# Layer 1's short scan: one length for each set of four states, and all sets of a group in one tile

## The chip, the cores and the metric

The kernel runs on one core of a Trainium2 chip. The metric is device time in microseconds. Three runs of the kernel before gave 12742.89, 12820.02 and 12823.61 us; their median is 12820.02 us.

Five engines work side by side, each through its own instructions in order, and wait for one another by semaphores: PE (matrix multiply, its results go to PSUM), DVE (vector operations and scans), ACT (activations and copies), POOL (vector operations on SBUF) and SP, which issues most of the DMA transfers here.

## The reference

Two layers of a state space model in two dimensions work on 8 images of 64 x 64 positions and 96 channels. Both normalize the image by groups, project it to 192 channels, convolve 3 x 3 by channel, and scan the 4096 positions in four directions with 16 states for each channel. A gated projection and a sum follow. Layer 0 has an ordinary recurrence. Layer 1 computes its scan by cumulative sums:

```python
dt = softplus(dt @ dt_proj_w + dt_proj_b)
A = -exp(A_log)                      # rates 1 to 16 in each channel
log_dA = einsum('bld,dn->bldn', dt, A)
dB_u = einsum('bld,bln->bldn', dt, B_mat) * u[..., None]
decay = exp(cumsum(log_dA, axis=1))
h = decay * cumsum(dB_u / (decay + 1e-12), axis=1)
y = einsum('bldn,bln->bld', h, C_mat) + u * D_skip
```

`decay` falls from position to position until it underflows to zero; from there on `h` is zero and only `u * D_skip` is left. So only the head of each of the four directions has to be scanned. How long the head must be depends on the sum of dt and on the rate of the state.

## The kernel before

**The long scan.** For layer 0, a step is one *set*: 4 of the 16 states of 32 channels on the 128 partitions, over 1024 positions. Four sets (`NS`) with the same channels are a *group*, three groups a *job* (96 channels, half `h`), and two jobs a *unit* (1024 positions in one direction). One image has 16 units, that is 384 sets.

`scan_rows` emits the work of all engines by hand, one set number n after another. For set n, DVE makes the drive and scans (`advance_set`); ACT makes the decay of set n+1 into PSUM (`fill`); POOL multiplies the states of set n-1 by C (`read_out`); PE sums the states of set n-3 into PSUM (`collect`); ACT takes the finished sums out (`release`). In the last set of a long group, POOL makes the drive instead of DVE (`early`, by `by_gpsimd`). SP fetches a group's replicated dt and dt*u from DRAM five sets ahead (`fetch`; two buffers each), and the rows of B and C four sets ahead (`replicate`; nine buffers in all). What prepares a job two jobs ahead (`ready`, `short_ready`) and the convolutions of other images (`conv_beside`) hang in a plan by set number; the numbers in the lists that these functions return are steps after the job's start. The matmuls of all planned stages share one bank (`pmisc`).

**The short scan.** Behind the long scan of images 1 to 7 stands one more unit, `short`: layer 1's scan of the image before. It scans a head of `HEAD` = 160 positions in each of the four directions. The four heads lie in one row of 640 columns (`HN`). The two heads of the backward directions are scanned from right to left, so that two scan instructions of 320 columns do a set; at the two joins dt is set to 1e30, which makes the decay zero there. The drive is first multiplied by 1 + tanh(...) of the summed dt (`gate`, and L838 in `advance_set`); this and the later factor 0.5 take the place of the division. The short unit has 2 jobs of 3 groups of 4 sets: 24 steps.

`short_ready` prepares a short job. It computes dt by softplus in several ACT steps, multiplies by u on POOL (`product`), sums dt along each head on DVE (`running`, L732, four scans of 160 columns into the buffer `dt0`), and keeps in `worst` the smallest product of a head's sum and the smallest rate (`lowest`). `store` at step 15 writes dt, dt*u and the sums to DRAM.

`worst` is compared with 104.5 (`GONE`) at the end of the program. If it is lower, a general scan of layer 1 is run for all images (`general_second`).

After the scan of an image, `between` finishes both layers' outputs (`out_phase`), where the matrix `avg` is loaded anew each time; the short scan's results come from DRAM (`ys_far`). The last image's layer 1 is done by `scan_head`, outside `scan_rows`.

Of the kernel before, what the change touches and what calls it, by code (L numbers as in the profile page):

```python
# [13 lines left out]
LATE = "in0", "in1", "cw0", "cw1", "cb0", "cb1", "spread", "avg", "pick"  # L14
# [24 lines left out]
CUTS = slice(0, MM), slice(MM, HN)  # L39

# [7 lines left out]
def two_ss2d_layers(ctx: ExitStack, tc: tile.TileContext, t: dict, out: bass.AP):  # L48
# [45 lines left out]
    nc.gpsimd.memset(one_col, 1.0)  # L94
    log_eps = const.tile([P, 1], F32, name="log_eps")
# [286 lines left out]
    def scan_parts(b):  # L382
# [20 lines left out]
        if b >= 1:  # L403
            unit = dict(short=True, nth=None, n=HN, b=b - 1)
            units.append(unit)
            for h in range(NH):
                jobs.append(dict(unit=unit, h=h))
                for g in range(NG):
                    group = dict(unit=unit, job=jobs[-1], h=h, g=g)
                    sets += [dict(unit=unit, group=group, i=i, first=False) for i in range(NS)]  # L410
# [3 lines left out]
    def scan_rows(xc, y, parts, plan, rows, beside):  # L414
# [10 lines left out]
        with (  # L425
# [11 lines left out]
            with tc.manual_schedule():  # L437
                state = None
                plan.setdefault(-1, []).insert(0, lambda: low_rows(x_dbl, units[1], rows))
                for n in range(-AHEAD, max(total + 4, max(plan, default=0) + 1)):  # L440
# [14 lines left out]
                    fetch(at(AHEAD), loads, work)  # L455
                    replicate(at(AHEAD_BC), x_dbl, loads)
                    if at(0) and at(0)["unit"]["nth"] == 0 and at(0)["first"]:
                        state = piece.tile([P, D // GC * NS], F32, name="state0", bufs=2)
# [3 lines left out]
                    if n % NS == NS - 2:  # L462
                        drive(at(2), pdrive)
                    release(at(-4), y, beside)
# [8 lines left out]
    def fetch(s, loads, work):  # L473

        if s and s["i"] == 0:
            group, n = s["group"], s["unit"]["n"]
            for c in ("dt", "dtu", "cum") if s["unit"]["short"] else ("dt", "dtu"):
                pool, size = (work, HN) if c == "cum" else (loads, T)
                group[c] = pool.tile([P, size], F32, name=f"{c}_rep")[:, :n]
# [3 lines left out]
    def replicate(s, x_dbl, loads):  # L483

        if s and s["group"]["h"] == 0 and s["group"]["g"] == 0:
            unit, n = s["unit"], s["unit"]["n"]
            if unit["short"]:
                rows, first = unit["far"], R
            else:
                rows = x_dbl[unit["k"] % 2][unit["k"] // 2 * ROWS :, unit["t0"] : unit["t0"] + T]  # L490
                first = R + 1
            for c, at in (("b", first), ("c", first + N)):
                rep = loads.tile([P, T], F32, tag="bc_rep", name=f"{c}_rep", bufs=2 * NS + 1)
                src = rows[at + GS * s["i"] :, :][:GS, :]
                nc.sync.dma_start(rep[:, :n], src.unsqueeze(0).broadcast_to([GC, GS, n]))
                unit[c, s["i"]] = rep[:, :n]
# [144 lines left out]
    def short_projection(xc, x_dbl, unit, piece, pmisc):  # L641


        def product(s):
            unit["ps"] = pmisc.tile([P, MM], F32, tag="mm", name="ps_short")
            at = CUTS[s]
# [9 lines left out]
        def take(s):  # L656
            if s == 0:
                unit["x_dbl"] = piece.tile([2 * ROWS, T], F32, name="x_dbl0")
            at, m = CUTS[s], R + 2 * N
            nc.scalar.copy(unit["x_dbl"][:m, at], unit["ps"][:m, : at.stop - at.start])  # L660
            if s == len(CUTS) - 1:
                unit["far"] = dram.tile([m, HN], F32, name="x_dbl1_short", bufs=2)
                nc.sync.dma_start(unit["far"], unit["x_dbl"][:m, :HN])
# [8 lines left out]
    def short_ready(xc, x_dbl, job, piece, pmisc):  # L672

        unit, h = job["unit"], job["h"]

        def bank(s, name):
            job["ps"] = pmisc.tile([P, MM], F32, tag="mm", name=name)
            return job["ps"][:C, : CUTS[s].stop - CUTS[s].start]

        def tile_of(name):  # L680
            return piece.tile([C, T], F32, name=name)[:, :HN]

        def argument(s):
            job["v"] = bank(s, "ps_dt1")
            lhs = w["dtw1"][:, 0, h * C : (h + 1) * C]
            nc.tensor.matmul(job["v"], lhs, unit["x_dbl"][:R, CUTS[s]], start=True, stop=True)

        def parts(s):
# [3 lines left out]
            nc.scalar.activation(job["dt"][:, CUTS[s]], job["v"], AF.Relu, bias=bias)  # L692
            nc.scalar.activation(job["z"][:, CUTS[s]], job["v"], AF.Abs, bias=bias)
# [15 lines left out]
        def total(s):  # L709
            job["v"] = bank(s, "ps_sp1")  # L710
            for i, term in enumerate(("z", "dtu", "ln", "dt")):
# [3 lines left out]
                    job[term][:, CUTS[s]],  # L715
# [4 lines left out]
        def delta(s):  # L720
            nc.scalar.copy(job["ln"][:, CUTS[s]], job["v"])
# [4 lines left out]
        def running():  # L726
            job["cum"] = tile_of("dt0")
            for k in range(K):
                d = slice(k * HEAD, (k + 1) * HEAD)
                if k >= 2:  # L730
                    d = slice(d.stop - 1, d.start - 1, -1)
                nc.vector.tensor_tensor_scan(  # L732
                    job["cum"][:, d],
                    one_col.to_broadcast([C, HEAD]),
                    job["ln"][:, d],
                    0.0,
                    ALU.mult,
                    ALU.add,
                )

        def lowest():
            last = small.tile([C, K], F32, name="last_short")
            for half in range(2):
                at = slice(HEAD - 1, 2 * HEAD, HEAD) if half == 0 else slice(2 * HEAD, HN, HEAD)
                nc.vector.tensor_scalar(
                    last[:, 2 * half : 2 * half + 2],
                    job["cum"][:, at],
                    w["least1"][:, h : h + 1],
                    None,
                    ALU.mult,  # L750
                )
# [4 lines left out]
        def store():  # L756

            nc.gpsimd.memset(job["ln"][:, JOINS], 1e30)
            job["dt"] = job["ln"]
            for c in ("dt", "dtu", "cum"):  # L760
                job[f"{c}_far"] = dram.tile([C, HN], F32, name=f"{c}_short", bufs=3)
# [7 lines left out]
            (3, exponential),  # L769
            (4, rounded),  # L770
            (5, rounding),
            (6, logarithm),
            (10, lambda: total(0)),
            (11, lambda: delta(0)),
            (11, lambda: total(1)),
# [1121 lines left out]
```

## Time and profile before

| What | Value |
|---|---|
| Median of 3 runs | 12820.02 us |
| Profiled execution, its own time | 12769.01 us |
| Its span in the profile | 12767.2 us |
| Instructions | 135071 |
| DVE busy | 11381.4 us (89%) |
| POOL busy | 10760.4 us (84%) |
| ACT busy | 9761.7 us (76%) |
| PE busy | 9506.2 us (74%) |
| Mean granted clock of PE | 0.788 |
| DMA queue of SP | 1818.14 MB, 43.2% of 16 engines |

All times in the profile come from the one profiled execution. A line such as L838 is a line of the kernel before. A group's line ends with the idle time of the engine just before its instructions, and with what ended that idle time. The lines of the order of instructions begin with the start and the length of an instruction in us; `<-` names output and input, and brackets hold an idle time and what ended it.

### The profile page before, as it was taken

Reading aid. Unit: us, or ns where it says so; the run is one execution under the profiler, and the core shown is the slowest. Engines: PE = TensorE matmul, PEld = TensorE weight load, DVE = VectorE, ACT = ScalarE, POOL = GpSimd, SP = SyncE. Lnnn points to the kernel's source line nnn. Section 1 sums busy time; section 2 is a strip of 40 time slices with the busy share of each in tenths; the row PEclk is TensorE's granted clock in tenths of the full one; section 3 lists DMA queues with packets and bytes.
Section 4 is the critical chain, followed back from the end, with each engine's and each line's share of the span. In section 5 each row is a group of like instructions: output and inputs, shape, how many; then the busy total and the mean of one; then the engine's idle time right before and its main releaser. Section 6 shows DMA issues by size and latency. Waiting matters only on the chain. (4 is left out here: it accounts for less than half of the span.)

```text
span 12767.2 us, 135071 instructions
## 1 busy us (share of the span) xinstructions
PE 9506.2 (74%) x44284; PEld 2996.9 (23%) x44284; DVE 11381.4 (89%) x7387; ACT 9761.7 (76%) x14977; POOL 10760.4 (84%) x4884
## 2 busy tenths in 40 slices
PE   5875588876887778876788758888588885886556
PEld 1221122222222222222222212222122221222112
DVE  6999799997999979999799987999889998899976
ACT  4888688776887768887788867888678886788864
POOL 3999799986999869998799977999779997899964
PEclk8877788777888778887788878878688877887766
DMA  3444444443444444444444435444344443444430
GB/s 97 161 161 155 133 164 162 160 139 117 164 161 160 142 128 164 156 156 132 133 161 161 158 119 155 150 152 159 122 151 161 159 152 117 146 159 159 153 98 25
DMA packets 653802, 1839.49 MB, mean 144 GB/s; under 512 B 174408, under 2 KB 177870, under 8 KB 652989
## 3 DMA queue, kind: packets, MB, share of 16 engines
q1 hardware_dynamic: 645917, 1818.14, 43.2%
q10 hardware_dynamic: 7168, 12.59, 0.3%
q8 instruction: 352, 5.77, 0.2%
q14 instruction: 365, 2.99, 0.1%
HBM read 1524.94 MB, written 305.52 MB: 143 GB/s over the span
## 5 line engine op out<-in xcount | busy, mean ns | idle before, releaser
L863 POOL TENSOR_TENSOR out<-set,c_rep 128x1024 f32<-128x1024 f32 x3240 | 7467.8, 2323 | 977.9 <-DVE set L846 307.5
L846 DVE TENSOR_TENSOR_SCAN set<-decay,state,set 128x1024 f32<-128x1024 f32 x2304 | 5365.2, 2345 | 390.1 <-ACT decay L801 151.6
L801 ACT ACTIVATE decay<-dt_rep,w_a 128x1024 f32<-128x1024 f32 x3240 | 3553.5, 1097 | 574.9 <-DVE set L846 334.5
L835 DVE TENSOR_TENSOR set<-drive,b_rep 128x1024 f32<-128x1024 f32 x2430 | 2865.2, 1179 | 15.9 <-ACT drive L818 9.0
L887 PE MATMUL acc<-out,w_gather 128*32 128x256 f32 x25920 | 2393.2, 481 | 546.8 <-ACT y_short L907 394.5
L955 PE MATMUL ps_conv<-edged,taps 96*96 96x512 f32 (+1 forms) x4032 | 2460.1, 749 | 29.8 <-ACT z L569 26.1
L825 POOL TENSOR_TENSOR set<-dtu_rep,b_rep 128x1024 f32<-128x1024 f32 (+1 forms) x810 | 1896.4, 2341 | 75.3 <-DMA dt_far<-ln 30.0
L846 DVE TENSOR_TENSOR_SCAN set<-decay,set 128x1024 f32<-128x1024 f32 x768 | 1744.3, 2286 | 167.7 <-ACT decay L801 87.8
L878 PE MATMUL acc<-map,w_eye 96*32 96x256 f32 x4608 | 566.8, 573 | 1471.7 <-ACT map L918 1237.3
L918 ACT COPY map<-acc 32x256 f32<-32x256 f32 x3072 | 1469.6, 478 | 48.3 <-PE acc L887 7.7
L887 PEld LDWEIGHTS acc<-out,w_gather 128*32 128x32 f32 x25920 | 839.4, 132 | 2519.4 <-issue 1455.0
L955 PEld LDWEIGHTS ps_conv<-edged,taps 96*96 96x96 f32 (+1 forms) x4032 | 722.8, 199 | 1371.0 <-issue 1230.3
L857 ACT COPY state<-set 128x1 f32<-128x1 f32 x2304 | 426.2, 185 | 752.1 <-DVE set L846 745.0
L588 PE MATMUL ps_sp<-z,w_eye 96*96 96x512 f32 x960 | 657.5, 773 | 292.7 <-ACT ln L597 245.0
L609 POOL TENSOR_TENSOR dtu<-ln,map 96x1024 f32<-96x1024 f32 x256 | 670.5, 2619 | 232.6 <-DVE ln L605 132.1
L818 ACT COPY drive<-dtu_rep 128x1024 f32<-128x1024 f32 (+1 forms) x810 | 797.2, 984 | 33.4 <-DVE x_in L1559 13.4
L556 PE MATMUL ps_dt<-x_dbl,w_dtw 7*96 7x512 f32 x1024 | 595.6, 663 | 219.6 <-ACT z L569 151.7
L588 PE MATMUL ps_sp<-dtu,w_eye 96*96 96x512 f32 x960 | 561.0, 669 | 0.0
L878 PEld LDWEIGHTS acc<-map,w_eye 96*32 96x32 f32 x4608 | 101.7, 122 | 1929.7 <-ACT map L918 1631.5
L588 PE MATMUL ps_sp<-ln,w_eye 96*96 96x512 f32 x960 | 540.8, 647 | 0.0
L588 PE MATMUL ps_sp<-dt,w_eye 96*96 96x512 f32 x960 | 507.8, 611 | 0.0
L597 ACT COPY ln<-ps_sp 96x512 f32<-96x512 f32 x480 | 278.7, 581 | 279.0 <-PE ps_sp L588 272.0
(228 smaller groups left out, 9621.6 us busy)
## 6 DMA issues: line engine op xcount, KB each, us to landing
dt_rep<-dt_far SPq DMA_DIRECT2D x768, 512.0 KB
dtu_rep<-dtu_far SPq DMA_DIRECT2D x768, 512.0 KB
b_rep<-x_dblr SPq DMA_DIRECT2D x256, 512.0 KB
c_rep<-x_dblr SPq DMA_DIRECT2D x256, 512.0 KB
b_rep<-x_dblc SPq DMA_DIRECT2D x256, 512.0 KB
c_rep<-x_dblc SPq DMA_DIRECT2D x256, 512.0 KB
dt_far<-ln SPq DMA_DIRECT2D x256, 384.0 KB
dtu_far<-dtu SPq DMA_DIRECT2D x256, 384.0 KB
```

Of the source, the lines that this page charges most:

```text
L588: nc.tensor.matmul(job["ps"][:C, :], w["eye"], job[term][:, halves[s]], start=i == 0, stop=i == 3,)
L609: nc.gpsimd.tensor_tensor(like(job["dtu"], col), like(job["dt"], col), positions(xc[:, h, :], col, t0, T), ALU.mult,)
L801: nc.scalar.activation(s["decay"], s["group"]["dt"], AF.Exp, scale=rate)
L818: nc.scalar.copy(s["group"]["drive"], s["group"]["dtu"])
L825: nc.gpsimd.tensor_tensor(s["buf"], s["group"]["dtu"], b, ALU.mult)
L835: nc.vector.tensor_tensor(s["buf"], s["group"]["drive"], b, ALU.mult)
L846: nc.vector.tensor_tensor_scan(ordered(s["buf"], unit), ordered(s["decay"], unit), ordered(s["buf"], unit), 0.0 if unit["nth"] == 0 else s ...
L863: nc.gpsimd.tensor_tensor(s["out"], s["buf"], s["unit"]["c", s["i"]], ALU.mult)
L878: nc.tensor.matmul(acc, lhs[:, GC * g : GC * (g + 1)], positions(old[:, h, :], unit["column"], unit["t0"] + at, n), start=True, stop=False ...
L887: nc.tensor.matmul(acc, w["gather"], s["out"][:, at : at + n], start=s["i"] == 0 and unit["short"], stop=s["i"] == NS - 1, skip_group_chec ...
L918: nc.scalar.copy(yk, like(acc, unit["column"]))
L955: nc.tensor.matmul(job["ps"][:C, :], taps[l][:k, h, tap, :], edged[:k, tap // 3 : tap // 3 + rows, tap % 3 : tap % 3 + WW], start=tap == 0 ...
```

## The change

Each set of four states gets a head of its own: 160, 40, 24 and 16 positions (`HEADS`). The smallest rate is taken for each set too (`least1`), so that the test of `worst` covers each set with its own length.

- The heads of all four sets of a group lie in one tile of 960 columns (`HT`): two halves of 480 (`BLOCK`), one for the forward and one for the backward directions; in each half the two heads of 160, then the two of 40, of 24 and of 16. A group of the short unit is now one step, not four: the unit has 6 steps.
- Decay and tanh use a different rate for each set, so ACT makes each of them in four pieces (`blocks`). The drive, the gated product, the two scans (480 columns each) and the read-out each do the whole tile. In the short unit the drive is always made by DVE.
- The ends of the convolved image are copied once more into the places of the shorter heads (`extend`, 12 small ACT copies per image). The projections and softplus of the short unit work on 960 columns.
- `running` uses two scans of 320 columns with a tile that has a zero at the second head's start. The products in `lowest` move from DVE to ACT (8 small ones per job).
- The stages of `short_ready` move up: `store` stands at step 11. It sets seven joins on POOL, where it was one instruction.
- Fetches of the short unit are issued two steps ahead; the sums use the buffers of B and C. B and C are loaded by four DMAs each.
- PE sums the four sets of a group by 16 matmuls of 160 to 16 columns. `release` is one ACT copy per group, and four stores to DRAM.
- For images 1 to 6 the convolutions beside the two last long jobs start at step 9.
- `avg` stays in SBUF.

The diff, cut to its core:

```diff
-LATE = "in0", "in1", "cw0", "cw1", "cb0", "cb1", "spread", "avg", "pick"
+LATE = "in0", "in1", "cw0", "cw1", "cb0", "cb1", "spread", "pick"
...
+HEADS = HEAD, 40, 24, 16
+OFFSETS = [2 * sum(HEADS[:i]) for i in range(len(HEADS))]
+BLOCK = 2 * sum(HEADS)
+HT = 2 * BLOCK
...
-                    sets += [dict(unit=unit, group=group, i=i, first=False) for i in range(NS)]
+                    sets.append(dict(unit=unit, group=group, i=0, first=False))
...
-                    fetch(at(AHEAD), loads, work)
+                    fetch(at(AHEAD), False, loads)
+                    fetch(at(2), True, loads)
                     replicate(at(AHEAD_BC), x_dbl, loads)
+                    replicate_short(at(AHEAD_BC), "b", loads)
+                    replicate_short(at(AHEAD_BC - 1), "c", loads)
...
-                    if n % NS == NS - 2:
-                        drive(at(2), pdrive)
-                    release(at(-4), y, beside)
+                    drive(at(2), False, pdrive)
+                    drive(at(1), True, pdrive)
+                    release(at(-4), y, work)
...
+    def blocks(ap, i):
+        return ap.rearrange("p (d a) -> p d a", d=2)[:, :, OFFSETS[i] :][:, :, : 2 * HEADS[i]]
+    def place(i, k):
+        start = k // 2 * BLOCK + OFFSETS[i] + k % 2 * HEADS[i]
+        return slice(start, start + HEADS[i])
...
+    def extend(ap):
+        pairs = ap.rearrange("p (d a) -> p d a", d=2)
+        for i in range(1, NS):
+            for d in range(2):
+                src = pairs[:, d, : 2 * HEAD].rearrange("p (k a) -> p k a", a=HEAD)
+                dst = blocks(ap, i)[:, d, :].rearrange("p (k a) -> p k a", a=HEADS[i])
+                nc.scalar.copy(dst, src[:, :, head_of(i, 2 * d)])
...
+    def replicate_short(s, c, loads):
+        if s and s["unit"]["short"] and s["group"]["h"] == 0 and s["group"]["g"] == 0:
+            unit = s["unit"]
+            rep = loads.tile([P, T], F32, tag="bc_rep", name=f"{c}_rep", bufs=2 * NS + 1)
+            unit[c, 0] = rep[:, :HT]
+            at = R if c == "b" else R + N
+            for i in range(NS):
+                src = blocks(unit["far"][at + GS * i :, :][:GS, :], i)
+                nc.sync.dma_start(
+                    blocks(unit[c, 0], i), src.unsqueeze(0).broadcast_to([GC, *src.shape])
+                )
...
-        def running():
+        def running(s):
+            if s == 0:
+                job["cum"] = tile_of("dt0")
+            at = slice(0, 2 * HEAD)
+            if s == 1:
+                at = slice(BLOCK + 2 * HEAD - 1, BLOCK - 1, -1)
+            nc.vector.tensor_tensor_scan(
+                job["cum"][:, at], ones_reset, job["ln"][:, at], 0.0, ALU.mult, ALU.add
+            )
...
-            nc.gpsimd.memset(job["ln"][:, JOINS], 1e30)
+            for i in range(NS):
+                for j in (OFFSETS[i], OFFSETS[i] + HEADS[i]):
+                    if j > 0:
+                        nc.gpsimd.memset(job["ln"][:, j : j + BLOCK : BLOCK - 1], 1e30)
...
             (3, exponential),
+            (4, logarithm),
             (4, rounded),
             (5, rounding),
-            (6, logarithm),
-            (10, lambda: total(0)),
-            (11, lambda: delta(0)),
-            (11, lambda: total(1)),
-            (12, lambda: delta(1)),
-            (13, product),
-            (13, running),
-            (14, lowest),
-            (15, store),
+            (6, lambda: total(0)),
+            (7, lambda: delta(0)),
+            (7, lambda: total(1)),
+            (8, lambda: delta(1)),
+            (9, product),
+            (9, lambda: running(0)),
+            (9, lambda: running(1)),
+            (10, lowest),
+            (11, store),
...
         if s["unit"]["short"]:
-            rate = w["a1"][:, column(s) : column(s) + 1]
+            for i in range(NS):
+                rate = w["a1"][:, column(s) + i :][:, :1]
+                src = blocks(s["group"]["dt"], i)
+                nc.scalar.activation(blocks(s["decay"], i), src, AF.Exp, scale=rate)
+            return
...
-            for d in (slice(0, 2 * HEAD), slice(HN - 1, 2 * HEAD - 1, -1)):
+            for d in (slice(0, BLOCK), slice(HT - 1, BLOCK - 1, -1)):
...
-            for k in range(K):
-                at = slice(k * HEAD, (k + 1) * HEAD)
-                acc = s["group"]["acc"][GC * k : GC * (k + 1), :HEAD]
-                nc.scalar.mul(unit["y"][GC * g : GC * (g + 1), h, at], acc, 0.5)
-            if (h, g) == (NH - 1, NG - 1):
-                ys_far[unit["b"]] = dram.tile([C, NH, HN], F32, name="ys_far", bufs=2)
-                nc.sync.dma_start(ys_far[unit["b"]], unit["y"])
+                ys_far[unit["b"]] = dram.tile([C, NH, HN], F32, name="ys_far", bufs=2)
+            part = work.tile([P, HEAD], F32, name="y_short", bufs=1)
+            nc.scalar.mul(part, s["group"]["acc"][:, :HEAD], 0.5)
+            dst = ys_far[unit["b"]][GC * g : GC * (g + 1), h, :]
+            for k in range(K):
+                at = slice(k * HEAD, (k + 1) * HEAD)
+                nc.sync.dma_start(dst[:, at], part[GC * k : GC * (k + 1), :])
...
+            if b >= 1 and m + NH >= K * NT * NH:
+                found.append((at + 9, (3, 3, 3), 1))
```

## The prediction

> **What bounds the kernel now.** I read the page's busy rows first, then the busy time of chosen stretches, then the groups by shape, then the order of instructions inside one short scan, and last who waited.
>
> ```profile
> span 12767.2 us, 135071 instructions
> PE 9506.2 (74%) x44284; PEld 2996.9 (23%) x44284; DVE 11381.4 (89%) x7387; ACT 9761.7 (76%) x14977; POOL 10760.4 (84%) x4884
> ```
>
> DVE leads, but this is an average. The stretches of image 1 (the long scan, then the short scan from its first product to its last scan, then the step between images; columns: length, busy time and instructions of PE, its loads, DVE, ACT, POOL, then clock, DMA share, GB/s):
>
> ```profile
> 1600.00:2877.66 1277.66, 1037.60 (x5010) 322.93 (x5010) 1212.68 (x699) 1036.40 (x1610) 1171.79 (x505) 0.81 0.47 156
> 2877.66:2973.10 95.44, 18.65 (x220) 9.33 (x224) 85.18 (x99) 51.28 (x79) 54.58 (x33) 0.50 0.20 66
> 2909.99:2924.36 14.37, 2.53 (x32) 1.32 (x32) 12.93 (x16) 8.35 (x14) 8.68 (x6) 0.50 0.21 68
> ```
>
> The short scan lasts 95.44 us with DVE 89% busy, and occurs 7 times (the last scans of the seven lie 1532 to 1579 us apart). A group of four sets takes 14.37 us; six groups are 86 us, and the first one is stretched.
>
> The groups by shape (xcount | busy, mean ns | idle before):
>
> ```profile
> L863 POOL TENSOR_TENSOR out<-set,c_rep 128x640 f32<-128x640 f32 x168 | 277.6, 1652 | 259.9 <-DVE set L841 231.5 <-issue 28.0 <-ACT y_short L907 0.3
> L841 DVE TENSOR_TENSOR_SCAN set<-decay,set 128x320 f32<-128x320 f32 x336 | 258.2, 810 | 5.8
> L838 DVE SCALAR_TENSOR_TENSOR set<-out,set 128x640 f32<-128x640 f32 x168 | 188.1, 1120 | 64.2 <-ACT out L812 55.4
> L835 DVE TENSOR_TENSOR set<-drive,b_rep 128x640 f32<-128x640 f32 x126 | 100.6, 798 | 0.0
> L801 ACT ACTIVATE decay<-dt_rep,w_a 128x640 f32<-128x640 f32 x168 | 133.4, 794 | 241.0 <-DVE set L841 180.9 <-issue 46.6 <-ACT out L812 7.0
> L812 ACT ACTIVATE out<-cum_rep,half_log,a_half 128x640 f32<-128x640 f32 x168 | 153.2, 912 | 36.8 <-issue 28.7 <-POOL out L863 6.8 <-PE acc L887 1.2
> L732 DVE TENSOR_TENSOR_SCAN dt<-one_col,ln 96x160 f32<-96x160 f32 x56 | 101.5, 1869 | 0.0
> ```
>
> The gated product L838 averages 1120 ns but takes 0.80 or 1.54, and L732 takes 1869 ns for 160 columns where L841 takes 810 for 320. The order of DVE's instructions shows it:
>
> ```profile
> 2906.06 1.54 DVE L838 SCALAR_TENSOR_TENSOR set<-out,set 128x640 f32<-128x640 f32 x1
> 2907.64 1.54 DVE L841 TENSOR_TENSOR_SCAN set<-decay,set 128x320 f32<-128x320 f32 x2
> 2909.09 0.80 DVE L835 TENSOR_TENSOR set<-drive,b_rep 128x640 f32<-128x640 f32 x1
> ...
> 2913.03 0.80 DVE L838 SCALAR_TENSOR_TENSOR set<-out,set 128x640 f32<-128x640 f32 x1
> ```
>
> Last, a wait before the short scan, while its second job (half h=1) is prepared:
>
> ```profile
> 2844.36 0.68 ACT L692 ACTIVATE dt<-ps_dt,w_dtb 96x512 f32<-96x512 f32 x1 [18.50 <-DMA cum_short<-dt]
> ...
> 2846.66 2.35 DVE L846 TENSOR_TENSOR_SCAN set<-decay,state,set 128x1024 f32<-128x1024 f32 x1 [5.15 <-ACT decay L801]
> ```
>
> ACT stood 18.5 us for the store of the first job's sums, because both jobs use one buffer and that store comes at step 15 where a job lasts 12 sets. DVE lost 5.15 us to it. This wait recurs: 126.2 us over 7 images.
>
> **The short scan, set by set to group by group.** 24 steps of 640 columns become 6 of 960. For one new step I scale by columns:
> - DVE: product L835 0.80 x 1.5 = 1.2 at most, and by the line through 640 (0.80) and 1024 (1.20) 1.13; two scans, 1.54 x 1.5 = 2.31; gated product 0.80 x 1.5 = 1.13 to 1.2. Together 4.6.
> - ACT: decays of 640 and 1024 columns take 794 and 1114 ns, so 0.833 ns a column and 0.26 fixed; four pieces are 0.80 + 4 x 0.26 = 1.84. Tanh likewise 0.80 + 4 x 0.38 = 2.32. Copy 0.95, release 0.30. Sum 5.4, or 4.9 if neighbours overlap by 0.1 as at 2844.36 (0.68 long, the next one begins 0.58 later).
> - POOL: read-out between 1.54 (640) and 2.36 (1024): 2.2.
> - DMA: three replicated tiles of 480 KB, 1.47 MB. The best stretches here moved 339 to 351 GB/s: 4.3 us.
>
> How these combine turns on the gated product. The Trainium skill, "SBUF — State Buffer", section "SBUF: two separate sides", says the SBUF port pair shared by DVE and GpSimd is an exclusive lock for a whole instruction, if the DVE operation has two SBUF inputs; the loser blocks. In the trace the 1.54 us product at 2906.06 ended 0.68 after POOL's read-out (2905.38 to 2906.92). By the lock, POOL takes the pair when a scan ends, DVE makes L835 meanwhile, and a step is 2.2 + 1.5 x 0.68 + 2.31 = 5.55. By the row's mean, L838 costs 1.68 and a step is 5.1. I take 5.55, since the next set of the old scan already alternates like this; ACT (4.9 to 5.4) and DMA (4.3) fit under it. Six steps: 33.3.
>
> The start: the second job is stored only 3 steps ahead of its first fetch, and dt and dtu have two buffers. SP issues in order: the stores wait for seven memsets on POOL, and the fetch of the second group stands behind them. Stores of 1.1 MB (3.3 us) and three fetches put the second group's sums about 1 us late. Bounds 0 and 8; I take 2.
>
> B and C rows are now loaded in pieces: 1536 runs of 128 to 320 bytes and 512 of 1280 per image, where eight loads of 2560-byte runs were. The Trainium skill, "DMA: Bandwidth & Descriptors", lists 512 B as the least transfer for line rate, with read-modify-write below, which speaks against this. The nearest row is the load of the convolution's input in 256-byte runs: at 2684 to 2686 the DMA share is 0.81 at 188 GB/s; less the replicate that had begun, its 960 runs took about 20 ns of one engine each. By that, 1536 runs cost 1536 x 0.02 / 16 = 2 us; at the mean packet's time (43.2% of 16 x 12767 us over 645,917 packets, 0.137 us) 13. They are issued four steps (about 20 us, with the sums' wait) ahead. I take 0, hidden by the last long sets; without that cover 2 to 13.
>
> **The preparation.** The sums become two scans of 320 instead of four of 160, both inputs in SBUF. Old cost per job 101.5/14 = 7.25, almost all wait for POOL: one job's first scan took 6.35 and the rest 0.46 to 0.52; in others each took one POOL instruction. New: 2 x 0.8 plus one or two waits, between 1.6 and 9 (POOL's product grows from 1.7 to 2.5); I take 6. The minimum keeps 1.5 on DVE (before 2.5 with its two multiplies; eight small ACT instructions replace these, about 1.6 us). So 7.5 a job, for both jobs before the scan.
>
> The compression to 11 steps stores the sums two sets before the next job overwrites the buffer, so the 18.5 us wait on ACT goes: 5.15 on DVE. What is late next: the last convolution is moved to step 9, its product reads the one PSUM bank at step 13, and the next job's first matmul waits for that at step 12. Behind it on PE is the gather, behind ACT's reading of it the decay of the set after next; about 0.5 to 2 us.
>
> Other work: twelve copies for the extended ends, 2.6 us of ACT; wider activations and copies, about 7 us of ACT; both lie under the long scan, where ACT is 81% busy. I charge 1 with the bank wait, and 3 if this cover were gone.
>
> **The end.** Six releases of one copy and four stores replace six of four copies and one store. Only the last matters: SP issues three more DMAs, 1.2 us. On the other side the averaging matrix is kept: the first mean could start 4.8 us after the last scan instead of 8.0 (POOL's sums end at 2977.33, PE's first mean starts at 2981.12). Between +2 and -3; I take 0.
>
> **Sum.** One image before: 95.44, plus the first job's 7.61 + 2.51 + 5.15 = 15.3: 110.7. After: 33.3 + 2 + 15 + 1 = 51.3. Gain 59.4, times 7: 416. The profiled execution took 12769 (span 12767.2), so 12353. The median of the runs is 51 above it; the same gain from 12820 gives 12404.
>
> **The rivals.**
> 1. Sum as worked out: 70%, 12350 to 12470.
> 2. Better: POOL gives the pair to the sums sooner (5 us an image), ACT sets the step at 4.9 (4), and the earlier mean counts (3): 12 x 7 = 84, 12320. For it: some L838 run in 0.80. Against: POOL starts its read-out 0.1 after a scan. 13%.
> 3. Transfers or ACT set the short step. Fetches, stores and small runs share 16 engines; at 8 us a step and 8 more at the start the loss is 23 x 7 = 160: 12565. Against: 4.3 us of bytes. 13%.
> 4. Slower: the short scan becomes one serial chain. If SP fetches a group only after the previous one is done, a step is issue and landing 6.1 (before: 4.7 from first issue for 0.98 MB), ACT 5.4, products and scans 4.6, read-out 2.2: 18.3. With 8 at the start and the 15 of preparation, 133 against 110.7: +156, or 12976. It decides from a step of 14.6, and passes 1% at 17.7. Against: two buffers, and no releases on SP until the fetches are issued. 3%.
> 5. The change does less than it says: a length test fails at run time and the general scan is run for all images. Sets with rates from 5, 9, 13 over 40, 24, 16 positions must reach 104.5; with small weights the step is about ln 2, giving 139, 150, 144 where the old test has 111. 1%, many milliseconds.
>
> **How the numbers follow.** The likeliest is 12404. The range leaves out half of case 2 and of case 3, and 4 and 5: 12320 to 12540. About 1% (128 us) is what a measurement here tells from no change; cases 1 and 2 and most of 3 lie beyond it: faster 0.93, same 0.03, slower 0.04.
>
> **What would show it.** First product to last scan of the short scan at 33 to 40 us; L838 near 2.2 us under a read-out; the 18.5 us wait absent; sums at 2 to 4 us each. If the short scan shows DVE idle behind tanh or a DMA, case 3 holds and the start is where I erred; if the long scan before it grows, the moved convolution or the added ACT work did.

## The result and the profile after

The changed kernel takes 12617.18 us, the median of four runs (12603.55 to 12623.85), where four runs of the kernel before, three of them those named at the start, have a median of 12804.64 (12742.89 to 12823.61). The ratio is 0.986, with a 95% interval of 0.982 to 0.990. A second series gave 12622.86 and again 0.986. So the change makes the kernel faster by 1.4%, 187 us, and not by the 416 that the prediction expected; the way was right and the size was not: 12617 lies above its range, which ended at 12540.

The head of the page and the engines' busy times after the change:

```profile
span 12613.3 us, 134470 instructions
PE 9519.2 (75%) x44284; PEld 3021.0 (24%) x44284; DVE 11031.8 (87%) x6870; ACT 9693.0 (77%) x15131; POOL 10513.1 (83%) x4802
```

DVE lost 350 us of busy time, but the span lost only 154. The stretches of image 1 show the long scan, the short scan from its first product to its last scan, and one group in the middle (columns as in the prediction):

```profile
1610.00:2897.09 1287.09, 1050.72 (x4978) 323.23 (x4976) 1213.11 (x694) 1043.89 (x1644) 1172.72 (x518) 0.81 0.47 156
2897.09:2938.54 41.45, 13.94 (x136) 9.19 (x136) 29.61 (x25) 30.97 (x60) 13.51 (x6) 0.54 0.54 192
2910.45:2916.06 5.61, 0.00 (x0) 0.00 (x0) 5.47 (x5) 5.51 (x12) 2.21 (x1) 0.50 1.00 357
```

One group takes 5.61 us where four sets took 14.37, close to the 5.55 worked out. Its gated product ended 1.02 us after the read-out beside it:

```profile
2911.69 2.22 DVE L895 SCALAR_TENSOR_TENSOR set<-out,set 128x960 f32<-128x960 f32 x1
2910.68 2.21 POOL L920 TENSOR_TENSOR out<-set,c_rep 128x960 f32<-128x960 f32 x1 [3.40 <-DVE set L898]
```

But the short scan as a whole takes 41.45 us, and DVE is busy for only 29.61 of them. The groups by shape (count | busy, mean ns | idle before) name what DVE waits for:

```profile
L781 DVE TENSOR_TENSOR_SCAN dt<-ones_reset,ln 96x320 f32<-96x320 f32 x28 | 106.3, 3835 | 0.8 <-PE ps_sp L760 0.8
L920 POOL TENSOR_TENSOR out<-set,c_rep 128x960 f32<-128x960 f32 x42 | 93.0, 2214 | 158.9 <-DVE set L898 138.1 <-ACT out L869 20.5 <-ACT drive L875 0.3
L898 DVE TENSOR_TENSOR_SCAN set<-decay,set 128x480 f32<-128x480 f32 x84 | 92.5, 1143 | 1.4
L895 DVE SCALAR_TENSOR_TENSOR set<-out,set 128x960 f32<-128x960 f32 x42 | 65.1, 1551 | 81.9 <-ACT out L869 80.6
L892 DVE TENSOR_TENSOR set<-drive,b_rep 128x960 f32<-128x960 f32 x42 | 47.8, 1139 | 5.0 <-ACT drive L875 5.0
L869 ACT ACTIVATE out<-cum_rep,half_log,a_half 128x640 f32<-128x640 f32 x42 | 38.6, 919 | 45.5 <-POOL out L920 45.4
L974 ACT ACTIVATE y_short<-acc 128x160 f32<-128x160 f32 x42 | 12.6, 299 | 93.0 <-DMA ys_far<-y_short 70.4 <-PE acc L933 19.5 <-PE ps_mean L1516 2.9
```

DVE stands 80.6 us for the tanh (L869), that is 11.5 an image. The tanh itself stands 45.4 us, and the row puts this down to POOL's read-out. The order of instructions says otherwise:

```profile
2921.95 2.22 POOL L920 TENSOR_TENSOR out<-set,c_rep 128x960 f32<-128x960 f32 x1 [3.42 <-DVE set L898]
2924.77 2.02 ACT L869 ACTIVATE out<-cum_rep,half_log,a_half 128x640 f32<-128x640 f32 x4 [3.26 <-POOL out L920]
```

The read-out had ended 0.60 us before this tanh began. What ended 0.09 us before it is PE's gather of the first group (the sum over its states; 2921.61 + 3.07 = 2924.68, shown below), which reads a tile of the tanh's output ring `out`; the ring has four buffers, and this is the fifth tanh. The sixth follows the second gather in the same way (2933.01, then 2933.10), and so do both in image 2. The release (L974) stands 70.4 us for the stores of the group before.

The loss outside the short scan is found by cutting the trace at the scans, which gives the following stages (means over images 1 to 7; for the stretch to the next image over the six that there are):

| Stage | before, us | after, us | difference |
|---|---|---|---|
| last 15 sets of the long scan, with the preparation | 63.9 | 68.5 | +4.6 |
| from there to the first short scan | 2.9 | 6.3 | +3.4 |
| first short scan's start to last one's end | 92.3 | 35.8 | -56.5 |
| from there to the next image's first scan | 157.6 | 169.6 | +12.0 |
| first 13 sets of that long scan | 43.5 | 52.7 | +9.2 |
| sets 14 to 369 | 1201.2 | 1203.8 | +2.6 |

The sum is -24.7 an image. The work after the last short scan, to the end of the program, went from 433.1 to 456.5 us, and what stands ahead of image 1's long scan grew by 6.7. With these the stages add up to the 154 us of the spans. Sets 14 to 369 took between 1196.5 and 1205.9 us as a mean in all kernels of this study, without a pattern; so a difference of a few us an image there is not given to any cause. The 9.2 us are a mean too: image 1's long scan, which follows an image without a short scan, began as late before the change as after (52.9 and 51.8 us for its first 13 sets); in images 2 to 7 it is 11.0.

### The profile page after: what moved, and what is told of

Same layout as the page of the kernel before. It is cut to its first block, busy times and chain, and to the rows that moved or that the text cites. A ratio compares the mean times of both kernels' runs of the same rounds, so it can differ in the third digit from the quotient of the medians.

```text
span 12613.3 us, 134470 instructions
## 1 busy us (share of the span) xinstructions
PE 9519.2 (75%) x44284; PEld 3021.0 (24%) x44284; DVE 11031.8 (87%) x6870; ACT 9693.0 (77%) x15131; POOL 10513.1 (83%) x4802
## 5 line engine op out<-in xcount | busy, mean ns | idle before, releaser
L920 POOL TENSOR_TENSOR out<-set,c_rep 128x1024 f32<-128x1024 f32 x3114 | 7290.0, 2360 | 954.3 <-PE acc L956 305.2
L856 ACT ACTIVATE decay<-dt_rep,w_a 128x1024 f32<-128x1024 f32 x3072 | 3419.3, 1114 | 298.5 <-DVE set L903 292.6
L892 DVE TENSOR_TENSOR set<-drive,b_rep 128x1024 f32<-128x1024 f32 x2346 | 2812.5, 1199 | 44.1 <-DMA b_rep<-x_dblr 33.6
L1023 PE MATMUL ps_conv<-edged,taps 96*96 96x512 f32 (+1 forms) x4032 | 2418.1, 739 | 30.3 <-ACT z L615 27.8
L956 PE MATMUL acc<-out,w_gather 128*32 128x256 f32 x24576 | 2285.0, 482 | 21.4 <-POOL out L920 21.3
L882 POOL TENSOR_TENSOR set<-dtu_rep,b_rep 128x1024 f32<-128x1024 f32 x768 | 1809.5, 2356 | 99.0 <-DMA b_rep<-x_dblr 47.5
L986 ACT COPY map<-acc 32x256 f32<-32x256 f32 x3072 | 1470.9, 479 | 46.6 <-PE acc L956 6.0
L956 PEld LDWEIGHTS acc<-out,w_gather 128*32 128x32 f32 x24576 | 784.6, 131 | 1954.4 <-issue 1256.1
L614 ACT ACTIVATE dt<-ps_dt 96x512 f32<-96x512 f32 x512 | 303.0, 592 | 276.8 <-PE ps_dt L602 257.3
```

What stands on the lines that cost most here:

```text
L856: nc.scalar.activation(s["decay"], s["group"]["dt"], AF.Exp, scale=rate)
L882: nc.gpsimd.tensor_tensor(s["buf"], s["group"]["dtu"], b, ALU.mult)
L892: nc.vector.tensor_tensor(s["buf"], s["group"]["drive"], b, ALU.mult)
L920: nc.gpsimd.tensor_tensor(s["out"], s["buf"], s["unit"]["c", s["i"]], ALU.mult)
L956: nc.tensor.matmul(acc, w["gather"], s["out"][:, at : at + n], start=False, stop=s["i"] == NS - 1, skip_group_check=True,)
L986: nc.scalar.copy(yk, like(acc, unit["column"]))
```

## The experiments

The theory after reading the two traces named three separate causes: the chain of release copies and stores (A), the place of a buffer (B) and the ring of tanh tiles (C). A fourth (D), that the gathers' lag is counted in steps, came out of the first runs. The rivals were that transfers set it all (T), and that removed waits only turn up in the next stage (O). The table gives the median, the ratio to the kernel before, and four stages. The kernels ran in four series, each beside its own runs of the kernel before, with medians of 12777 to 12805. The ratios allow for this; differences of medians from different series do not, and so are good to some 30 us.

| Kernel | us | ratio | short scan | to the next scan | first 13 sets | last 15 sets |
|---|---|---|---|---|---|---|
| before | 12805 | 1 | 92.3 | 157.6 | 43.5 | 63.9 |
| after | 12617 | 0.986 | 35.8 | 169.6 | 52.7 | 68.5 |
| after, again | 12623 | 0.986 | 35.8 | 172.5 | 53.4 | 69.0 |
| own columns | 12556 | 0.981 | 35.7 | 167.9 | 53.0 | 68.6 |
| ones moved | 12507 | 0.978 | 35.8 | 166.0 | 43.3 | 69.1 |
| in place | 12581 | 0.983 | 32.3 | 174.1 | 53.1 | 68.4 |
| these three | 12441 | 0.972 | 32.3 | 163.8 | 42.6 | 68.5 |
| before, with pad | 12869 | 1.006 | 92.4 | 164.8 | 52.8 | 64.1 |
| short lags | 12530 | 0.980 | 30.5 | 169.4 | 52.7 | 69.0 |
| three and lags | 12421 | 0.972 | 30.5 | 161.0 | 43.5 | 68.2 |
| and sums from PSUM | 12382 | 0.969 | 30.6 | 159.1 | 42.8 | 60.7 |
| and ACT order | 12448 | 0.974 | 33.6 | 164.7 | 42.7 | 61.7 |
| whole rows | 12616 | 0.987 | 35.8 | 171.7 | 52.8 | 68.8 |

**Where a buffer lies.** The change added small constants that live for the whole program, the largest of them `ones_reset` with 1280 bytes a partition. They push up what is allocated later: worked out from the tiles' sizes, the final stage's third `sz` tile moved from bytes 171264-175360 to 173024-177120, and the first `dt_rep` buffer of the next long scan lies at 176096-180192. In the trace of the changed kernel, SP's first fetch for image 2 goes out 3.0 us before DVE's last addition of the final stage ends (3098.75, against 3101.76); in the kernel before it was 24.7 us ahead (3098.44 against 3123.09). SP's waits of the changed kernel (us in total, times, longest) have a new row, once for each of the six borders:

```profile
SPq L518 <- PE ps_r L1521: 123.3, 6, 21.4
```

Two runs tell whether that is the cause: one takes the overlap out of the changed kernel, the other puts it into the kernel before.

```diff
-    ones_reset = const.tile([C, 2 * HEAD], F32, name="ones_reset")
...
+                ones = w["ones_reset"] = pool.tile([C, 2 * HEAD], F32, name="ones_reset")
```

> The changed kernel, with the row of ones and zeros (1280 bytes a partition) taken from the kernel-wide constants into the tile pool that lives only for a scan. The final stage's third buffer then ends at byte 175840, below the first buffer of replicated steps (176096), as it did before the change. Theory B (the overlap makes the next long scan's first loads wait for the final stage): the first 12 sets of a long scan, 50.5 us now, go back to about 41, and 3 us more at its first product; 12.6 x 7 = about 85, time about 12530. Rival T (transfers in general are slower after the change): 12617.

```diff
+            pad = pool.tile([C, 320], F32, name="pad")
+            nc.gpsimd.memset(pad, 1.0)
```

> The kernel before, with 1280 unused bytes a partition added ahead of the final stage's buffers, and nothing else. They end then at byte 176640, past 176096 where the first buffer of replicated steps begins. Theory B (that overlap alone makes the next long scan's loads wait): the first 12 sets of a long scan go from 43.5 to about 53 us as in the changed kernel, 12 x 7 = 84, time about 12880, slower than before by 0.6%. Rival T (the loads are late for another reason that came with the change): as before, 12800.

Both went as theory B said. With the row of ones moved the first fetch is 24.7 us ahead again (3089.68 against 3114.33), and with the pad it is 3.0 (3141.61 against 3144.61). Moving the row won 110 us by the medians; the pad alone cost the kernel before 0.6% (interval 0.3 to 0.8%). The order of DVE's instructions at the start of image 2's long scan, first after the change, then with the row of ones moved, then before with the pad:

```profile
3106.53 1.23 DVE L892 TENSOR_TENSOR set<-drive,b_rep 128x1024 f32<-128x1024 f32 x1 [4.77 <-DMA b_rep<-x_dblr]
...
3126.16 2.29 DVE L903 TENSOR_TENSOR_SCAN set<-decay,set 128x1024 f32<-128x1024 f32 x1 [11.17 <-ACT decay L856]
```

```profile
3115.83 1.23 DVE L889 TENSOR_TENSOR set<-drive,b_rep 128x1024 f32<-128x1024 f32 x1 [1.50 <-ACT drive L872]
3117.16 2.29 DVE L900 TENSOR_TENSOR_SCAN set<-decay,set 128x1024 f32<-128x1024 f32 x1
3119.36 1.20 DVE L889 TENSOR_TENSOR set<-drive,b_rep 128x1024 f32<-128x1024 f32 x1
```

```profile
3149.00 1.23 DVE L835 TENSOR_TENSOR set<-drive,b_rep 128x1024 f32<-128x1024 f32 x1 [4.39 <-DMA b_rep<-x_dblr]
...
3167.47 2.29 DVE L846 TENSOR_TENSOR_SCAN set<-decay,set 128x1024 f32<-128x1024 f32 x1 [10.23 <-ACT decay L801]
```

The waits of 4.77 and 11.17 us go with the overlap and come with the pad (4.39 and 10.23). SP's waits in the padded kernel show the same new row, at that kernel's line numbers:

```profile
SPq L481 <- PE ps_r L1446: 129.9, 6, 22.5
```

The stage table adds that the overlap also costs in the stretch ahead of the next scan: +7.2 with the pad, -3.6 to -6.5 without the overlap.

**The chain of releases.** `y_short` has one buffer. Here each release copy goes to its own columns of one tile:

```diff
-            part = work.tile([P, HEAD], F32, name="y_short", bufs=1)
+                unit["y"] = piece.tile([P, T], F32, tag="z0", name="y_short")
+            part = unit["y"][:, (h * NG + g) * HEAD :][:, :HEAD]
```

> The changed kernel (12617 us), with one difference: each of the six small release copies of the short scan goes to its own 160 columns of one tile, so none waits until the stores of the group before have landed. Theory A (the chain copy, four stores, landing, next copy holds the gathers and the first mean of the next stage): the stretch from the last short scan to the next image's first scan, 169.6 us now, falls by about 10, the 70 us of waits on these stores go, time about 12545. Rival T (the small DMA runs and the bytes moved in the short scan delay what follows): nothing changes, 12617.

The waits for the stores went (what the release waits for now is PE's gather, 64.1 us in all), but the stretch to the next scan fell by 1.7 to 4.6 us only. The rest of the 61 us that the median fell lies in sets 14 to 369 and behind the last short scan, where nothing is attributed. So theory A was too simple. The order on PE shows why, first after the change and then with own columns:

```profile
2921.61 3.07 PE L933 MATMUL acc<-out,w_gather 128*32 128x160 f32 x32 [15.58 <-ACT map L986]
2929.94 3.07 PE L933 MATMUL acc<-out,w_gather 128*32 128x160 f32 x32 [5.26 <-ACT y_short L974]
...
2946.76 1.73 PE L933 MATMUL acc<-out,w_gather 128*32 128x160 f32 x32 [2.80 <-ACT y_short L974]
```

```profile
2924.29 3.07 PE L933 MATMUL acc<-out,w_gather 128*32 128x160 f32 x32 [15.57 <-ACT map L987]
...
2946.07 1.73 PE L933 MATMUL acc<-out,w_gather 128*32 128x160 f32 x32 [0.49 <-ACT y_short L975]
```

Even with own columns PE cannot begin the first short gather until the last long group is released (ACT L986), which ends 19 us after the first short scan began. The rest of the six gathers then comes as a queue, and ends 6.6 us after the last short scan's end (2941.22), in place of 9.95. With it wait SP's other transfers: `map`, the first that the next stage needs, was issued 6.7 us after the last short scan in the kernel before, 15.8 after the change, 10.5 with own columns.

**The ring of tanh tiles.** The read-out goes in place over the states:

```diff
+            else:
+                s["out"] = s["buf"]
```

> The changed kernel, with the short read-out written in place over its states instead of over the tanh's tile, so that a tanh slot is free as soon as the gated product has read it. Theory C (tanh waits for a slot of a ring of four, twice about 4 us in each short scan): the short scan, 35.8 us from first to last scan now, goes to about 28 plus what the ports cost, 7.9 x 7 = about 55, time about 12560. Rival O (these waits lie beside the release chain and are only moved to it): the short scan shrinks but the stretch after it grows by as much, 12617.

Rival O holds at least in part: the short scan lost 3.5 us, and the stretch after it grew by 4.5 against the first run of the changed kernel and by 1.6 against the second. Of the 36 us by the medians the rest lies where nothing is attributed. The tanh no longer waits, but DVE does, since the `set` buffers are now held until the same late gather:

```profile
2910.21 1.16 DVE L892 TENSOR_TENSOR set<-drive,b_rep 128x960 f32<-128x960 f32 x1 [2.99 <-PE acc L935]
```

The three edits together:

> The three edits together (own columns, row of ones moved, read-out in place). If the three causes are separate their gains add: 70 + 85 + 55 = 210, time about 12405, near the forecast of 12404. If they cover one another (rival O: one wait ends where the next begins), less than the sum of the three single gains: 12450 to 12530.

They gave 12441: 176 us of the 210 that theory C, A and B added up to, and less than the sum of the three single medians' gains (61 + 110 + 36 = 207). So they cover one another in part, though the 31 us between 207 and 176 are little: the changed kernel's median comes from another series and enters the sum of the three gains three times.

**The lag in steps.** Both the release chain and the tanh ring depend on the late first gather. In the code of the change, a set is gathered three steps after its scan and released four steps after. A step was one set, and is now a group of four. The last long group's release therefore stands in ACT's order behind the activations of four short groups.

```diff
+                lag = lambda i: 2 if i >= last and last < total - 1 else 3
...
+                lag = lambda i: short if i > last else 4
...
-                    release(at(-4), y, work)
+                    for i in early_end(n, 3):
+                        release(sets[i], y, work)
...
-                    collect(at(-3), xc, y, pacc)
+                    for i in late_start(n):
+                        collect(sets[i], xc, y, pacc)
+                        if i == last:
+                            release(sets[i], y, work)
```

Here `last` is the last long set: it is gathered two steps after its scan and released right behind that; a short group is gathered at two and released at three.

> The changed kernel; the gather of a short group comes two steps after its scans instead of three, its release one step later, and the last long group's gather and release one and two steps earlier. All of these lags are counted in steps, and a step of the short scan grew from one set to a group. Theory D (the gathers are late because the last long group's release, which frees the one PSUM bank, is issued four groups into the short scan): the first short gather comes about 11 us earlier, so that tanh slots are free too, and both the tanh waits (3.5 in the short scan) and a part of the 12 us after it go: 6 to 10 an image, time 12550 to 12575. Theory A as it stood (the store landings alone hold the chain): no gain, 12617.

> The three edits of the kernel of 12441 us (own columns, row of ones moved, read-out in place) and the shorter lags. That kernel's short scan still had DVE wait 2.96 and 1.18 us for gathers, and its stretch to the next image's first scan was 163.8 against 157.6 us before. Theory D: both waits go and the last gather ends some 2 us earlier: 4 + 2 to 5 an image, 40 to 65 in all, time 12375 to 12400. Rival O (what is won only moves to the stage after): 12441.

The first run, with the lags alone, gave 12530, 93 us less than the unedited kernel beside it and more than expected. The groups by shape of that kernel:

```profile
L913 DVE SCALAR_TENSOR_TENSOR set<-out,set 128x960 f32<-128x960 f32 x42 | 71.1, 1692 | 35.9 <-ACT out L887 34.4
L887 ACT ACTIVATE out<-cum_rep,half_log,a_half 128x640 f32<-128x640 f32 x42 | 38.5, 916 | 0.4
L992 ACT ACTIVATE y_short<-acc 128x160 f32<-128x160 f32 x42 | 12.7, 301 | 80.9 <-DMA ys_far<-y_short 65.6 <-PE acc L951 15.2
```

The lags alone, with the ring as it was, took the tanh's wait for it from 45.4 to 0.4 us, which confirms that the gather held it, and DVE's wait for the tanh from 80.6 to 34.4; the short scan took 30.5. The stores' landings still hold the releases (65.6), and the stretch to the next scan shrank by 0.2 to 3.1 us only. Of the gain 37 us are the short scan's (5.3 x 7); the rest lies in stretches where nothing is attributed, or at the end of the program (443.7 after the last short scan). On top of the three edits the same lags gave 20 us by the medians, and no difference that the ratios can tell (0.972 for both). Theory D expected 40 to 65; the gathers came earlier, but the last one waits for POOL's last read-out in any case. In image 1 it began 2.43 us after the last short scan both times, and with the lags it ended later, at 5.4 in place of 4.2, since it took 2.97 us and not 1.76 (the last section says why such times differ).

**The running sums.** What is left is the preparation. Here the sums read dt from PSUM, where a matmul left it:

```diff
-                job["cum"][:, at], w["ones_reset"], job["ln"][:, at], 0.0, ALU.mult, ALU.add
+                job["cum"][:, at], w["ones_reset"], job["v"][:, of], 0.0, ALU.mult, ALU.add
...
+            (7, lambda: running(0)),
             (7, lambda: total(1)),
             (8, lambda: delta(1)),
+            (8, lambda: running(1)),
             (9, product),
-            (9, lambda: running(0)),
-            (9, lambda: running(1)),
```

> The kernel of 12421 us, with the running sums reading the step sizes from PSUM, where the matmul left them, and not from the copy in SBUF, each half right after its copy. Theory P (two scans with two SBUF inputs stood behind three POOL instructions for the shared ports: 7.3 us a job for two scans of 0.8): a sum takes 0.8 again, 5.7 less a job, 11.4 an image, time about 12340. Rival Q (ACT, which runs just ahead of DVE in this stretch, then ends last): DVE waits for decays instead, 12380 to 12421.

The group by shape of the kernel with lags, then of this one:

```profile
L796 DVE TENSOR_TENSOR_SCAN dt<-ones_reset,ln 96x320 f32<-96x320 f32 x28 | 105.1, 3792 | 0.0
```

```profile
L797 DVE TENSOR_TENSOR_SCAN dt<-ones_reset,ps_sp 96x320 f32<-96x320 f32 x28 | 22.8, 815 | 45.0 <-ACT ln L784 45.0
```

A scan fell from 3792 to 815 ns with one input moved to PSUM. The edit also moves the sums to an earlier step, so they might only have got away from POOL. They did not: all 28 scans ran under POOL instructions with SBUF inputs for at least 0.71 of their length, and 24 of them for 0.94 or more. Here are one of them and the read-out that it ran under:

```profile
2874.52 0.82 DVE L797 TENSOR_TENSOR_SCAN dt<-ones_reset,ps_sp 96x320 f32<-96x320 f32 x1 [0.76 <-ACT ln L784]
2873.91 2.35 POOL L938 TENSOR_TENSOR out<-set,c_rep 128x1024 f32<-128x1024 f32 x1 [1.21 <-PE ps_sp L775]
```

That is what the rule of the Trainium skill would make of it ("SBUF — State Buffer", section "SBUF: two separate sides": a DVE instruction with at most one SBUF input, outside the modes that use two ports, does not contend with GpSimd, the engine called POOL here). Theory P is right on the price, and rival Q on the end: 82 us less of scans, 45 us of new waits for ACT, and 39 us less time by the medians. The ratios, from two series, overlap (0.969 to 0.974 with lags, 0.967 to 0.971 here); what shows the gain is the stage, which lost 7.5 us an image. At 12382 us this is the fastest kernel of the study, at 0.969 (0.967 to 0.971) of the kernel before.

**The order on ACT.** The tanh goes ahead of the long group's release, and two small activations come one set later:

```diff
+                    if at(1) and at(1)["unit"]["short"]:
+                        gate(at(1), work)
                     for i in early_end(n, 3):
                         release(sets[i], y, piece)
...
-            (4, rounded),
-            (5, rounding),
+            (5, rounded),
+            (6, rounding),
```

> The previous kernel, with two changes of the order on ACT: the tanh of a short group is issued ahead of the release of a long group, and two of the preparation's small activations come one set later, away from the logarithm and its two table loads. Theory R (DVE's waits of 3.28 for the first tanh and 3.83 for a decay behind the table loads are a matter of the order on ACT): 2.4 and 1 an image less for both, about 20 to 30 in all. Rival: the same work only waits elsewhere, 0.

It took 12448, 66 us more. The wait ahead of the first short scan fell from 6.3 to 3.8 us, but the second group then waited for ACT, where the release copies now stood behind the first tanh:

```profile
2901.82 1.16 DVE L911 TENSOR_TENSOR set<-drive,b_rep 128x960 f32<-128x960 f32 x1 [1.85 <-ACT drive L894]
2903.71 2.32 DVE L914 SCALAR_TENSOR_TENSOR set<-out,set 128x960 f32<-128x960 f32 x1 [0.73 <-ACT out L888]
```

The short scan grew by 3.0 us and the stretch after it by 5.6. The same work only waits elsewhere, and longer.

**The small runs.** B and C of the short scan are fetched in whole rows of 3840 bytes, not in pieces:

```diff
-            for i in range(NS):
-                src = blocks(unit["far"][at + GS * i :, :][:GS, :], i)
...
+            src = unit["far"][at:, :][:GS, :]
+            nc.sync.dma_start(unit[c, 0], src.unsqueeze(0).broadcast_to([GC, GS, HT]))
```

> The changed kernel, but B and C of the short scan are fetched by one transfer each of whole rows of 3840 bytes, those of the first set for all four (it leaves out the rows of the other three sets). Rival T (the 2048 small runs an image delay what is behind them): up to 13 us an image less, 12530. Mine (they lie four steps ahead, off the path): 12617, within 30.

12616, with every stage as in the changed kernel. Rival T falls as far as these small runs go: they are not on the path, though the DMA engines are full in the middle of the short scan (share 1.00 at 357 GB/s in the row above).

## Why the prediction was wrong

The prediction had 59.4 us an image, the runs 24.7. It had the cost of a step right. It failed on what stands around the steps: it took 0 for the end, 2 for the start and 1 for the waits of the preparation, and it had no term for the place of the buffers. Step by step:

- **The short step: right.** Expected 5.55 (its sum as written gives 5.53), measured 5.61; scans 2.20 for two (2.31 expected), gated product 2.22 to 2.25 under a read-out, products 1.13. The 1.02 us by which the product outlasted POOL's read-out (2913.91 against 2912.89) are the 1.5 x 0.68 of the prediction, so this was no luck. ACT did fit under it: while nothing held it, its tanh came every 4.68 us (2904.78, 2909.46, 2914.14). The DMA engines were full (share 1.00), but no wait of DVE or ACT in this short scan was ended by a transfer.
- **"The start ... I take 2": too low.** The first tanh came 3.28 us late, behind ACT's release copies of a long group. And two more waits of 3.99 and 3.89 us, in the fifth and sixth group, have no term: only one step was costed, and whether the ring of four is free when the lags grow with the step was not asked. First product to last scan took 41.45 us in place of 35.3: 6.2 lost. The prediction named DVE idle behind the tanh as the sign of case 3. It came, but the tanh was held by the late gather and the release copies, not by ACT's own time or by transfers.
- **"I charge 1 with the bank wait": too low.** Before the first product the stretch grew by 5.4 us where 0.7 was expected: 4.7 lost. The 15 for sums and minima held as a sum (15.3), with two errors that cancel: the sums took 7.44 and 7.30 us, not 6, and the minimum 0.3, not 1.5. The wait of 18.5 us on ACT went as predicted, and DVE's 5.15 with it. In its place DVE waits 3.83 (for a decay behind the logarithm and two table loads), 0.36 and 0.66 (for the first drive), and 2.36 just ahead of this stretch.
- **"The end ... between +2 and -3; I take 0": wrong.** It grew by 12.0. Only the issue of three more stores was counted; not that the gathers start 19 us into the short scan, that each release waits for the stores before it, and that the next stage's transfers stand behind all of these on SP. The runs share out the 12.0 only roughly: 3.6 to 7.2 for the buffer's place, 1.7 to 4.6 for the chain of releases; with all edits 1.5 to 3.4 are left. The kept matrix was worth nothing at first, since PE's first mean stands behind the gathers. With all edits that mean began 4.3 us after the last scan in place of 7.9, even earlier than the predicted 4.8, and the stretch was still 1.5 us longer than in the kernel before.
- **No term at all: the place of the buffers.** 9.2 us an image at the start of the long scans, and the part just named. The prediction counted the instructions of what the change adds, and not its bytes.

Together 6.2 + 4.7 + 12.0 + 9.2 and the 2.6 of sets 14 to 369 make 34.7, which is the difference. What the program lost behind the last short scan (23.4 us in all) comes on top; with all edits 6.0 of it are left (439.1 us). Rival 3 had the nearest number, 12565, but that was luck: transfers and ACT did not set the step. Undoing the named causes brings 377 us in place of 187 (12797.75 to 12421.08), and 395 with the faster sums (12776.68 to 12381.65). That this is near the 416 is in part chance, since the forecast did not contain those sums.

What stays open is what moves sets 14 to 369 by some us between kernels, and how the last 1.5 to 3.4 us of the stretch to the next scan come about.

## What to carry to other kernels

When work is packed into larger steps, every lag and every ring that is counted in steps grows too: go through what is issued several steps later, and ask which bank, ring or queue waits for it. A constant that is added costs its bytes: see which buffers of neighbouring stages it pushes over one another, since a prefetch of twelve transfers of 512 KB came 22 us late here for 1.3 KB a partition. A forecast for a step in the middle can be good to 1% and say little about the whole; the borders, from the last long group to the first short one and from there to the next stage, have to be costed with the same care.

## What the runs showed of the hardware

- The same gathers of a group took 3.07 us on PE at a granted clock of 0.50 and 1.73 at 1.00, a factor of 1.8. So it was with all 35 of the changed kernel's 42 that ran at one clock throughout (17 and 18 of them); the other seven, during which the clock changed, lie between. The idle time ahead of a gather does not decide it: the last one in the rows above came after 2.80 us and took 1.73. In these rows the clock stands third from the end; the gathers at 2929.94 and 2946.76 lie in the first and the second:

```profile
2928.20:2938.40 10.20, 6.07 (x64) 5.10 (x64) 6.28 (x6) 3.78 (x9) 2.21 (x1) 0.50 0.07 16
2938.50:2952.00 13.50, 7.08 (x100) 5.16 (x100) 2.39 (x3) 2.33 (x6) 6.08 (x5) 1.00 0.11 24
```

- With POOL instructions queued without a gap, a DVE scan with two SBUF inputs did not come between them: in the kernel with the three edits and lags POOL ran three from 2871.64 to 2878.45, and the first of two scans, begun at 2872.54, ended at 2879.14; the second took 0.79 us. In each of the 14 jobs of that kernel, and of the 14 of the changed kernel, one of the two scans took 6.6 to 7.4 us and the other 0.8.
- A round from one release copy to the next, which waits for the landing of four small stores, took 3.2 and 4.5 us in image 1 of the changed kernel (copies at 2938.56, 2941.78 and 2946.31), though the stores together are only 80 KB.
